# A two-layer relational graph convolution on one core: loop weights spread by DMA, both layers' edge weights from one product, one rotation of seven PSUM banks

## The chip, the cores and the metric

The kernel runs on one core of one Trainium2 chip. The core has five engines that work side by side, each through its own instructions in order: TensorE (PE; the profile lists its weight loads apart, as PEld), VectorE (DVE), ScalarE (ACT), GpSimd (POOL) and SyncE (SP), which here only issues DMAs. Engines wait for one another through semaphores. The metric is the device time of one execution in microseconds (us), lower is better.

## The reference

There are 50,000 nodes with 128 features, and 850,000 edges sorted by destination: 800,000 random ones and one self edge for each node. Every edge has one of 16 relations. Two layers follow each other, and the second has matrices of its own:

```python
W   = einsum('rb,bio->rio', w_comp, basis)         # 16 relations from 8 bases
agg = segment_sum(h[src], dst * 16 + rel, ...)     # sum of neighbours by node and relation
out = relu(einsum('nri,rio->no', agg, W) + h @ loop_w + bias)
```

The result is `layernorm(x + layer2(layer1(x)))`, all in float32. As the sums are linear, the kernel forms, for each node and each basis b, the sum over its edges of `w_comp[rel, b] * h[src]`, and multiplies that by the 8 basis matrices.

## The kernel before

**Edges.** The 800,000 real edges are cut into tiles of 128, 10 tiles to a chunk (`K`), 625 chunks in each layer. For each tile one indirect DMA on POOL (`gather`, line 247) fetches the 128 source rows into one of four row buffers of a chunk each (`GATHERS`); the gathers of chunk c+2 are issued in the code at chunk c, and a gather waits until the PE has read the tile that lay in its place, 40 tiles earlier. The PE multiplies the tile by a "hot" matrix of 128 edges x (8 bases x 12 nodes) (line 961), and DVE adds the 128 x 96 result into a ring of sums in SBUF, at an offset read from a table (`add`, line 897; the offsets come by a register load, line 891). Edge tile k is called slot k below. The adds of slot k stand in DVE's order `BEHIND` = 10 slots later. A bank of PSUM holds the products of five tiles (`PER`).

**Edge weights.** For every fourth chunk (`BATCH`) the class `Weights` loads relations and offsets (`load`, lines 632 and 636), compares them with each partition's relation on DVE (`compare`, line 648), multiplies the comparison by the layer's coefficients on the PE (`multiply`, line 655, five products of 64 columns) and copies the 320 columns to SBUF on ACT (`kept`, line 665, the single-buffered tile `pm`). `hot_of` makes the hot matrix of one chunk from `pm` (lines 870 and 877). All of this is done once in each layer.

**Groups of nodes.** Sums are taken out in groups of 512 nodes (`GN`), 98 in a layer, some 64 slots apart. The class `Group` first puts the self edge into the ring: `load` fetches the self edges' relations (line 685) and the node rows (line 694, turned on the PE, line 702, and copied by ACT, line 705) or, in layer 2, the columns stored by layer 1 (line 696); `compare` (line 713) makes a 96 x 512 comparison; then for each of the 8 bases `repeat` (line 720) multiplies it by a 96 x 128 matrix whose columns are all equal, so that every partition gets the weight of the basis for each node, and `own` (line 731) multiplies that bank of PSUM by the node's features into the ring. `planned` places the eight `repeat` steps `APART` = 5 slots apart, each `own` 10 slots behind its `repeat`. When all edges of a group are in, `copy` (line 748, ACT) takes 128 x 4096 sums out, `base` (line 754) multiplies them by the 8 basis matrices, three slots apart, `loop` (line 759) adds the self-loop matrix, `relu` (line 766) stores the columns, `back` (line 778) turns them, and `store` writes rows (layer 1, line 786) or normalizes and writes the output (layer 2).

**Order.** The order on PE, POOL, DVE and ACT is written out by hand: `later` puts a step at a slot, and the main loop runs the steps that are due. SP's order is left to a planner. Products go to two rotations of PSUM banks, `Turns`: `sums_a`, four banks, for the edge products, and `sums_o`, three banks, for everything else (`repeat`, `multiply`, `turn`, `back`). Whoever takes a bank waits until its earlier content has been read. An eighth bank holds the result of `base` and `loop`.

Of the kernel before, what the change touches and what calls it, by code (L numbers as in the profile page):

```python
# [76 lines left out]
BEHIND = 10  # L77
AFTER = 16
APART = 5
# [8 lines left out]
def tile_rgcn_resnorm(  # L88
# [43 lines left out]

    FULL = dram.tile([2 * NP, 2], F32, name="FULL")
# [17 lines left out]
    BASIS, LOOP, EACH, BIAS_OF, SPLIT = [], [], [], [], []  # L151
# [4 lines left out]
    def weighed():  # L156


        steps = consts.tile([P, AT - 1], F32, name="steps")
# [3 lines left out]
        passed = consts.tile([P, AT - 1], F32, name="passed")  # L163
        nc.vector.tensor_scalar(passed, steps, part, None, op0=OP.is_le)
        its_tile = consts.tile([P, 1], F32, name="its_tile")
# [3 lines left out]
        one_tile = consts.tile([P, AT], F32, name="one_tile")  # L169
        nc.vector.tensor_scalar(one_tile, col[:, :AT], its_tile, None, op0=OP.is_equal)  # L170
        which = consts.tile([P, PARTS], F32, name="which")
        nc.vector.tensor_scalar(which, col[:, :PARTS], its_tile, None, op0=OP.is_equal)
        again = consts.tile([P, PARTS], F32, name="again")
        nc.vector.tensor_scalar(again, col[:, PARTS : 2 * PARTS], its_tile, None, op0=OP.is_equal)
        nc.vector.tensor_add(which, which, again)
        for n, (basis, w_comp, loop_w, bias) in enumerate(GIVEN):
            bs = consts.tile([P, NB, D], F32, name=f"basis{n}")
            nc.scalar.dma_start(bs, basis.rearrange("b i o -> i b o"))
            BASIS.append(bs)
            lw = consts.tile([P, D], F32, name=f"loop{n}")  # L180
            nc.scalar.dma_start(lw, loop_w)
            LOOP.append(lw)

            ec = consts.tile([P, NB], F32, name=f"ec{n}")
# [3 lines left out]
            each = consts.tile([P, AT, NB], F32, name=f"each{n}")  # L188
            nc.vector.tensor_tensor(
                each,  # L190
# [4 lines left out]
            EACH.append(each)  # L195
# [4 lines left out]
            left, mine = ec, consts.tile([P, NB], F32, name=f"mine{n}")  # L200
            for i in range(PARTS):
                short = consts.tile([P, NB], BF16, name=f"short{n}{i}")
# [7 lines left out]
                if i + 1 < PARTS:  # L210
                    less = consts.tile([P, NB], F32, name=f"less{n}{i}")
                    nc.vector.tensor_tensor(less, left, short, op=OP.subtract)
                    left = less
            split = consts.tile([P, NB, P], BF16, name=f"split{n}")
            nc.vector.tensor_copy(split, mine[:, :, None].to_broadcast([P, NB, P]))
            SPLIT.append(split)

    ps_a = ctx.enter_context(tc.tile_pool(name="ps_a", bufs=4, space=PSUM))
    ps_o = ctx.enter_context(tc.tile_pool(name="ps_o", bufs=3, space=PSUM))
# [24 lines left out]
    sums_a, sums_o = Turns(ps_a, "pa", 4), Turns(ps_o, "po", 3)  # L244
# [6 lines left out]
    def turned(h, m, sb):  # L251

        tp = ps_o.tile([P, BANK], F32, name="po")
# [22 lines left out]
    ones = consts.tile([P, P], F32, name="ones")  # L276
# [183 lines left out]
    def rows_of(j, pool):  # L460
# [18 lines left out]
        def put(of, to):  # L479
            at = to[:, r0 * HALF : (r0 + m) * HALF].rearrange("e (r k) -> e k r", k=HALF)  # L480
            for k0 in range(0, HALF, BANK // P):
                n = min(BANK // P, HALF - k0)
                tp = sums_a.take()
# [47 lines left out]
        po = sums_o.take()  # L531
# [37 lines left out]
    def count_up(pool):  # L569
# [3 lines left out]
        total = sums_o.take()  # L573
# [26 lines left out]
    def chunked():  # L600
        with (
# [20 lines left out]
            class Weights:  # L622
# [5 lines left out]
                def load(self):  # L628
# [6 lines left out]
                    self.rel = hp.tile([P, LIVE], U8, name="rel")  # L635
# [14 lines left out]
                def multiply(self):  # L650
                    m = self.m
                    self.po = sums_o.take(self.keep)
                    of = self.po[:, :WEIGHTS].rearrange("e (t j) -> e t j", t=AT)
                    for j in range(PER):
                        nc.tensor.matmul(  # L655
                            of[:, :, j * NB : (j + 1) * NB],
                            self.is_rel[:m, j * P : (j + 1) * P],
                            EACH[self.n][:m],
                            start=True,
                            stop=True,  # L660
                        )

                def kept(self):
                    pm = hp.tile([P, WEIGHTS], F32, name="pm", bufs=1)
                    nc.scalar.copy(pm, self.po[:, :WEIGHTS])  # L665
                    self.pm = pm.rearrange("e (t b) -> e t b", b=NB)

            class Group:
                def __init__(self, g, of, n, copied):
# [3 lines left out]
                    self.each, self.made = {}, False  # L673
                    self.keep, self.kept = Once(self.turned), Once(self.store, 0)
                    self.owns = [Once(self.own, b) for b in range(NB)]

                def load(self):
                    g, n, m, cnt = self.g, self.n, self.m, self.cnt
                    if n == 0:
                        end = min(N, (g + 1) * GN)  # L680
                        while stored[0] < min(NG, -(-(end + NEAR) * E // (N * RUN * P))):
                            next(coming)
                        loaded[0] = end
# [7 lines left out]
                    self.hT = sb.tile([P, GN], F32, name="hT", bufs=4)  # L691
                    if n == 0:
                        self.h = sb.tile([P, J, D], F32, name="h_own")
                        nc.sync.dma_start(self.h[:m], of_group(self.of, g))
                    else:
                        nc.sync.dma_start(self.hT[:, :cnt], H1T[:, g * GN : g * GN + cnt])

                def turn(self):
                    m = self.m
                    self.po = sums_o.take(self.keep)  # L700
# [16 lines left out]
                def repeat(self, b):  # L717
                    cnt = self.cnt
# [465 lines left out]
```

## Time and profile before

| | |
|---|---|
| median of 3 runs (lowest to highest) | 18110.66 us (18107.38 to 18120.93) |
| profiled execution | 18092.07 us |
| its span, first to last instruction | 18090.2 us |
| mean granted TensorE clock | 0.609 |
| busy: POOL, PE, DVE, PEld, ACT | 68%, 49%, 38%, 37%, 7% |
| DMA | 1095.35 MB, mean 61 GB/s |

The profile is one execution. In its list of groups a row is: line, engine, operation, result<-operands, shape, count | busy us in all, mean ns of one | idle us of the engine just before them, and what ended most of that. "issue" is idle time in which the profile shows nothing that was waited for; "remote" is a wait whose end no recorded instruction explains. Rows of a timeline are: start in us, busy us, engine, line, operation, shapes, count, [idle before <- what ended it]. Rows of the waits are: engine and line, what it waited for, us in total, times, longest us.

### The profile page before, as it was taken

What the parts mean: (1) busy time and instruction counts of PE and PEld (TensorE: products, weight loads), DVE (VectorE), ACT (ScalarE), POOL (GpSimd) and SP (SyncE); (2) the same over time, 40 slices, a digit from 0 to 9 for tenths busy, and PEclk for the clock granted to TensorE, in tenths of its full rate; (3) what the DMA queues carried; (4) which work ended last, traced back from release to release, by engine and by line L of the source; (5) the groups of instructions that cost most, each with busy time, mean ns of one, the idle gap of its engine ahead of it and who ended that gap; (6) DMA issues with size and microseconds to landing.
All of it is one profiled execution on the core that took longest, in us unless ns stands there. A gap on an engine that the chain in (4) does not pass through costs nothing.

```text
span 18090.2 us, 137615 instructions
## 1 busy us (share of the span) xinstructions
PE 8815.7 (49%) x34524; PEld 6699.9 (37%) x34524; DVE 6821.1 (38%) x19683; ACT 1346.6 (7%) x1452; POOL 12297.6 (68%) x12540
## 2 busy tenths in 40 slices
PE   4444444544555444444444444444445444544445
PEld 3333333333333333333333333333333333333333
DVE  5444444444333333333333333333333333333333
ACT  0000000000000000000000000000000000000000
POOL 6666666666666666666666666666666666666666
PEclk6656666665665666666655666566565666666666
DMA  2222222222222222222222222222222222222222
GB/s 78 68 69 64 68 69 68 68 63 62 59 59 58 59 59 59 59 58 59 57 55 58 58 59 58 58 58 59 58 58 58 59 58 59 59 59 59 58 58 54
DMA packets 568561, 1095.35 MB, mean 61 GB/s; under 512 B 218506, under 2 KB 262764, under 8 KB 567756
## 3 DMA queue, kind: packets, MB, share of 16 engines
q0 software_dynamic: 403552, 826.82, 18.9%
q1 hardware_dynamic: 161276, 258.45, 4.4%
q8 instruction: 282, 4.62, 0.1%
q14 instruction: 523, 4.28, 0.1%
q10 hardware_dynamic: 2928, 1.19, 0.0%
HBM read 987.64 MB, written 97.93 MB: 60 GB/s over the span
## 4 chain that ended last, share of the span: by engine, by line
issue 39%; PE 28%; another core or an unknown queue 15%; DVE 8%; POOL 6%; DMA 2%; ACT 1%; DVEq 1%; POOLq 0%; ACTq 0%; SPq 0%
PE pa L961 16%; PE pn L754 7%; POOL g L247 6%; DVE ring L897 4%; PE po L655 2%; DVE ring L731 2%; PE po L720 1%; DMA g<-in_x_dram,src 1%; DVEq L891 1%; DMA g<-H,src 1%; ACT own L748 1%; PE po L778 1%; PE pn L759 1%; DVE own L870 0%
## 5 line engine op out<-in xcount | busy, mean ns | idle before, releaser
L961 PEld LDWEIGHTS pa<-hot,g 128*128 128x128 f32 x25000 | 5222.6, 274 | 8042.2 <-issue 7000.4
L247 POOL DMA_INDIRECT g<-in_x_dram,src x6250 | 6140.9, 983 | 2844.0 <-issue 1397.4
L247 POOL DMA_INDIRECT g<-H,src x6250 | 6120.1, 979 | 2864.0 <-issue 1410.5
L961 PE MATMUL pa<-hot,g 128*128 128x96 f32 x25000 | 5476.4, 355 | 4369.5 <-issue 3768.7
L897 DVE TENSOR_TENSOR ring<-pa,ring 128x96 f32 x12500 | 3205.9, 256 | 10795.4 <-remote 5049.8
L754 PE MATMUL pn<-own,basis 128*128 128x512 f32 x3104 | 2296.2, 818 | 529.6 <-issue 515.5
L720 PE MATMUL po<-is_lrel,split 96*128 96x512 bf16 x1568 | 797.8, 510 | 2312.8 <-issue 903.2
L877 DVE TENSOR_TENSOR hot<-pm,own 128x960 f32<-128x960 f32 x1250 | 1451.4, 1161 | 81.1 <-ACT pm L665 13.8
L655 PE MATMUL po<-each,is_rel 128*128 128x64 f32 x3140 | 671.9, 375 | 1159.1 <-issue 727.1
L731 DVE TENSOR_TENSOR ring<-po,hT 128x512 f32<-128x512 f32 x1568 | 1078.8, 689 | 110.8 <-remote 29.5
L655 PEld LDWEIGHTS po<-each,is_rel 128*128 128x128 f32 x3140 | 625.5, 289 | 1209.5 <-issue 747.3
L748 ACT COPY own<-ring 128x4096 f32<-128x4096 f32 x194 | 699.5, 3606 | 3877.3 <-DVE ring L897 2158.7
L754 PEld LDWEIGHTS pn<-own,basis 128*128 128x128 f32 x3104 | 668.4, 253 | 768.6 <-issue 766.5
L665 ACT COPY pm<-po 128x320 f32<-128x320 f32 x314 | 133.5, 425 | 6635.0 <-DVE hot L877 2743.9
L778 PE MATMUL po<-ident,oT 128*128 128x128 f32 (+1 forms) x784 | 205.6, 397 | 650.2 <-DVE ring L731 388.9
L778 PEld LDWEIGHTS po<-ident,oT 128*128 128x128 f32 (+1 forms) x784 | 143.8, 220 | 684.2 <-issue 537.3
L720 PEld LDWEIGHTS <-split 96*128 96x128 bf16 x1568 | 236.0, 151 | 388.0 <-issue 387.5
L766 ACT ACTIVATE oT<-pn,bias_of 128x512 f32<-128x512 f32 x196 | 134.7, 687 | 3019.6 <-PE pa L961 1597.5
L870 DVE TENSOR_TENSOR own<-col,key 128x120 bf16<-128x120 f32 x1250 | 346.4, 277 | 0.5
L759 PE MATMUL pn<-hT,loop 128*128 128x512 f32 x392 | 265.6, 759 | 32.5 <-issue 32.2
L326 DVE COPY_PREDICATED word<-bit,word 128x224 int32<-128x224 int32 (+9 forms) x450 | 181.2, 403 | 16.1 <-DVE bit L323 0.8
L648 DVE TENSOR_SCALAR is_rel<-rel,its_rel 128x640 f32<-128x640 uint8 x314 | 181.3, 578 | 0.1
(126 smaller groups left out, 1497.1 us busy)
## 6 DMA issues: line engine op xcount, KB each, us to landing
g<-in_x_dram,src POOLq DMA_INDIRECT x6250
g<-H,src POOLq DMA_INDIRECT x6250
lrel<-LREL SPq DMA_DIRECT2D x194, 192.0 KB
rel<-REL SPq DMA_DIRECT2D x312, 80.0 KB
h_own<-in_x_dram SPq DMA_DIRECT2D x97, 256.0 KB
xw<-in_x_dram SPq DMA_DIRECT2D x97, 256.0 KB
H1T<-oT SPq DMA_DIRECT2D x97, 256.0 KB
H<-t SPq DMA_DIRECT2D x97, 256.0 KB
```

Source lines behind the costliest of these rows:

```text
L247: return nc.gpsimd.indirect_dma_start(out=to, out_offset=None, in_=of, in_offset=bass.IndirectOffsetOnAxis(ap=idx, axis=0))
L655: nc.tensor.matmul(of[:, :, j * NB : (j + 1) * NB], self.is_rel[:m, j * P : (j + 1) * P], EACH[self.n][:m], start=True, stop=True,)
L720: nc.tensor.matmul(self.each[b][:, :cnt], SPLIT[self.n][:LOOPS, b, :], self.is_rel[:LOOPS, :cnt], start=True, stop=True,)
L731: nc.vector.tensor_tensor(ring[:, b, self.at : self.at + cnt], self.each.pop(b)[:, :cnt], self.hT[:, :cnt], op=OP.mult,)
L748: nc.scalar.copy(self.sums, ring[:, :, at : at + cnt])
L754: nc.tensor.matmul(self.pn[:, : self.cnt], BASIS[self.n][:, b, :], self.sums[:, b, :], start=b == 0, stop=False)
L759: nc.tensor.matmul(self.pn[:, : self.cnt], LOOP[self.n], self.hT[:, : self.cnt], start=False, stop=True)
L778: nc.tensor.transpose(self.po[:m, j * D : (j + 1) * D], by_place[:, j, :], ident)
L870: nc.vector.tensor_tensor(own[:, : ks(c)], grid[:, None, :].to_broadcast([P, ks(c), WN]), key[:, c * K : c * K + ks(c), None].to_broadcast ...
L877: nc.vector.tensor_tensor(hot[:, : ks(c)], pm[:, c % BATCH * K : c % BATCH * K + ks(c), :, None].to_broadcast([P, ks(c), NB, WN]), own[:, ...
L897: nc.vector.tensor_tensor(into, pa[:, k % PER * NB * WN : (k % PER + 1) * NB * WN].rearrange("d (b w) -> d b w", w=WN), into, op=OP.add,)
L961: nc.tensor.matmul(pa[:, k % PER * NB * WN : (k % PER + 1) * NB * WN], g[:, k, :], hot[:, k].rearrange("e b w -> e (b w)"), start=True, st ...
```

## The change

Self-edge weights: one product for each group, made in layer 1 alone, gives 16 rows (8 bases of both layers) x 512 nodes (`combine`). ACT copies them, SP stores them to DRAM (`CW`), and in both layers SP loads four bases at a time back, each row repeated over 128 partitions (`widen`, into a tile with a single buffer, `WIDE` = 1). `own` then multiplies four bases at once, from SBUF. Edge weights: in layer 1 each product has the columns of both layers (128 in place of 64) and fills two banks, ACT makes four copies, and the part of layer 2 goes to DRAM (`PM2`), from where layer 2 loads it; layer 2 makes no comparison and no product of its own. PSUM: one rotation of seven banks for all. `BASIS` and `LOOP` have one buffer and are loaded again for layer 2. `BEHIND` is 12 and `AFTER` is 18 (16 before); `base` steps are two slots apart. Core of the diff:

```diff
-BEHIND = 10
-AFTER = 16
-APART = 5
+BEHIND = 12
+AFTER = 18
+AT_ONCE = 4
+WIDE = 1
+PARTS_OF = ((0, 3), (3, 5))
...
-    sums_a, sums_o = Turns(ps_a, "pa", 4), Turns(ps_o, "po", 3)
+    banks = Turns(ps_a, "pa", 7)
...
 class Weights: def load
+    if self.n:
+        pm = hp.tile([P, WEIGHTS], F32, name="pm")
+        nc.sync.dma_start(pm, PM2[c // BATCH * P : (c // BATCH + 1) * P, :])
+        return
...
 def multiply
-    self.po = sums_o.take(self.keep)
+    self.po = [banks.take(self.keep) for _ in PARTS_OF]
...
 def kept
+    for n in range(2):
+        for po, (j0, j1) in zip(self.po, PARTS_OF):
+            nc.scalar.copy(...)
+        if n:
+            nc.sync.dma_start(PM2[c * P : (c + 1) * P, :], pm)
...
 class Group:
-    def repeat(self, b):
+    def combine(self):
+        nc.tensor.matmul(self.comb[: 2 * NB, : self.cnt],
+            split[:LOOPS].rearrange("r n b -> r (n b)"), self.is_rel[:LOOPS, : self.cnt], ...)
+    def stored_comb(self):
+        nc.scalar.copy(comb[:, :cnt], self.comb[: 2 * NB, :cnt])
+        nc.sync.dma_start(CW[:, at : at + cnt], comb[:, :cnt])
+    def widen(self, b):
+        self.wide[b] = sb.tile([P, AT_ONCE, GN], F32, name="wide", bufs=WIDE)
+        nc.sync.dma_start(self.wide[b][:, :, : self.cnt], bass.AP(tensor=CW.tensor, ...,
+            ap=[[0, P], [NGR * GN, AT_ONCE], [1, self.cnt]]))
     def own(self, b):
-        nc.vector.tensor_tensor(ring[:, b, ...], self.each.pop(b)[:, :cnt], self.hT[:, :cnt], op=OP.mult)
+        nc.vector.tensor_tensor(ring[:, b : b + AT_ONCE, ...], self.wide.pop(b)[:, :, :cnt],
+            self.hT[:, None, :cnt].to_broadcast([P, AT_ONCE, cnt]), op=OP.mult)
...
 def planned
-    went = start - APART * NB - BEHIND
-    later(went - 28, self.load)
-    for b in range(NB):
-        later(went + APART * b, self.repeat, b)
-        later(went + APART * b + BEHIND, self.owns[b])
+    went = start - 2
+    if self.n == 0:
+        later(went - 78, self.load)
+        later(went - 66, self.turn)
+        later(went - 62, self.compare)
+        later(went - 48, self.combine)
+        later(went - 48 + BEHIND, self.combined)
+    else:
+        later(went - 40, self.load)
+    for i, b in enumerate(range(0, NB, AT_ONCE)):
+        later(went - 30 + 14 * i, self.widen, b)
+        later(went - 16 + 14 * i, self.own, b)
-        later(end + AFTER + 3 * b, self.base, b)
+        later(end + AFTER + 2 * b, self.base, b)
...
+    if n:
+        later(30, matrices, 1, nc.sync)
```

More of the change, by code (lines that the diff above doesn't have):

```diff
@@ L690, in load @@
                     )
[L691 to L696, printed above, removed]
+                    self.h = sb.tile([P, J, D], F32, name="rows")
+                    nc.sync.dma_start(self.h[:m], of_group(self.of, g))
                 def turn(self):
                     m = self.m
-                    self.po = sums_o.take(self.keep)
+                    self.po = banks.take(self.keep)
                     for j in range(J):
```

183 lines of the change are left out of this document (103 added, 80 removed).

## The prediction

> **What bounds the kernel now.** I read the groups by cost first.
>
> ```profile
> span 18090.2 us, 137615 instructions
> L247 POOL DMA_INDIRECT g<-in_x_dram,src x6250 | 6140.9, 983 | 2844.0 <-issue 1397.4
> L247 POOL DMA_INDIRECT g<-H,src x6250 | 6120.1, 979 | 2864.0 <-issue 1410.5
> L877 DVE TENSOR_TENSOR hot<-pm,own 128x960 f32<-128x960 f32 x1250 | 1451.4, 1161 | 81.1 <-ACT pm L665 13.8
> L655 PE MATMUL po<-each,is_rel 128*128 128x64 f32 x3140 | 671.9, 375 | 1159.1 <-issue 727.1
> L731 DVE TENSOR_TENSOR ring<-po,hT 128x512 f32<-128x512 f32 x1568 | 1078.8, 689 | 110.8 <-remote 29.5
> L720 PE MATMUL po<-is_lrel,split 96*128 96x512 bf16 x1568 | 797.8, 510 | 2312.8 <-issue 903.2
> L778 PE MATMUL po<-ident,oT 128*128 128x128 f32 (+1 forms) x784 | 205.6, 397 | 650.2 <-DVE ring L731 388.9
> ```
>
> POOL's 12,500 gathers are the longest row. Next I read one gather by itself, from its source line, and its pace in a timeline.
>
> ```profile
> L247 POOL DMA_INDIRECT g<-in_x_dram,src x6250: 938/945/1929, 45.8 to 9064.3; - x196
> L247 POOL DMA_INDIRECT g<-H,src x6250: 938/945/1932, 9099.2 to 18049.3; - x196
> ```
> ```profile
> 12006.27 1.16 DVE L877 TENSOR_TENSOR hot<-pm,own 128x960 f32<-128x960 f32 x1
> 12006.54 1.71 POOL L247 DMA_INDIRECT g<-H,src  x1 [0.30 <-issue]
> ...
> 12017.29 0.95 POOL L247 DMA_INDIRECT g<-H,src  x1 [0.30 <-issue]
> 12018.54 0.94 POOL L247 DMA_INDIRECT g<-H,src  x1 [0.30 <-issue]
> ```
>
> Undisturbed, a gather starts every 1.25 us (0.95 and 0.30). POOL's floor is then 12,500 x 1.25 = 15,625; plus gathers stretched beyond their median, (983 - 945) x 6250 + (979 - 945) x 6250 ns = 450; plus 46 before the first, 35 between the layers (9064.3 to 9099.2) and 41 after the last: 16,197 us. The span is 18,090. So POOL spends about 1,890 us waiting, and that is all that any change which leaves the gathers alone can win. For whom does it wait?
>
> ```profile
> PEld pa L961 <- issue: 7000.4, 6266, 37.7
> POOL g L247 <- remote: 1229.4, 1060, 5.4
> POOL g L247 <- PE pa L961: 1204.3, 1538, 6.8
> PEld pa L961 <- DMA g<-in_x_dram,src: 221.3, 127, 17.4
> PEld pa L961 <- DMA g<-H,src: 201.4, 120, 17.9
> ```
>
> POOL waits for the PE to free row buffers, while the PE hardly waits for gathered rows (221 + 201). So the PE runs behind, with the 40 row tiles nearly full, and it sets the pace. It is not the PE's work: it idles 2312.8 + 1159.1 + 650.2 = 4,122 us before the three operations that take a bank of the three-bank rotation (L720, L655, L778 above). There is a second loss, which no wait explains. Timeline, start of layer 2:
>
> ```profile
> 9150.77 0.32 PE L961 MATMUL pa<-hot,g 128*128 128x96 f32 x1 [2.48 <-issue]
> ...
> 9152.18 0.29 PEld L961 LDWEIGHTS pa<-hot,g 128*128 128x128 f32 x1 [2.52 <-issue]
> ...
> 9153.57 0.32 PE L961 MATMUL pa<-hot,g 128*128 128x96 f32 x1 [2.48 <-issue]
> ```
>
> For tens of us the PE takes one instruction every 1.4 us, with nothing it waits for. Most of the 7,000 us "issue" above is of this kind; its cause I can't see.
>
> **The change part by part.** Sums are against the profiled span; the profiled execution (18,092.07) lies 2 above the span and 18.6 below the median.
>
> *`repeat` goes.* Off the PE: 1,568 products, 798 us, and the 2,313 idle before them; 98 `combine` products at some 0.5 us come in, 50.
>
> *Edge weights of layer 2 go.* Half of L655: (672 + 1,159) / 2 = 915 us of PE. Layer 1's products get 128 columns for 64. No row has that width in float32; the bounds are no change (375 ns) and L754's 128x512 float32 product at 818 ns, so 0 to (818 - 375) x 1,570 = 700 us; I take 100, near the lower end, because L961's 96 columns already cost no more (355 ns) than L655's 64:
>
> ```profile
> L754 PE MATMUL pn<-own,basis 128*128 128x512 f32 x3104 | 2296.2, 818 | 529.6 <-issue 515.5
> L961 PE MATMUL pa<-hot,g 128*128 128x96 f32 x25000 | 5476.4, 355 | 4369.5 <-issue 3768.7
> ```
>
> *Seven banks.* An edge bank is held 5 + 12 = 17 slots and was 5 + 10 = 15 of the four banks' 20. Layer 1 now takes, in 64 slots, 12.8 edge banks, 3.2 for weights and 3 for turn, combine and back: 7 of 19 is 23.6 slots. Layer 2 takes 13.8: 32.5 slots. DVE's slack rises from 5 slots to 6.6 and 15.5. Of what idles before L655 and L778 and is not yet counted, 580 + 650, I take half: 615. In all the PE is spared 3,111 - 50 + 915 - 100 + 615 = 4,490 us: its own path falls to some 13,600, below POOL's floor.
>
> *`own` on DVE.* 1,568 x 689 ns go (1,079). 392 operations of 128x2048, all operands in SBUF, come.
>
> ```profile
> L742 DVE TENSOR_TENSOR ring<-ring 128x96 f32<-128x96 f32 x64 | 16.5, 258 | 2.2
> ```
>
> From 96 to 960 columns (L742, L877) a column costs (1161 - 258) / 864 = 1.045 ns, so 2048 cost 2.30 us: 902 in all. DVE, busy for 6.8 ms, gains little; the cost is POOL's. L877 reads two SBUF operands, and the gather that starts under it above took 1.71 instead of 0.95. Charging all 450 us of stretch to L877's 1,451 busy us gives 0.31 us of POOL per us; for 902 that is 280. The ends are 0 and 902; I take 280, measured on the same kind of operation.
>
> The Trainium skill ("SBUF — State Buffer", section "Who interferes with whom") says that a DVE instruction with two SBUF inputs shares a read interface with GpSimd, and that the later of the two blocks fully until the other ends; one with a single SBUF input does not contend. The trace agrees in kind (1.71 us); a full block would charge 902, which is a rival below.
>
> *Other work moved.* ACT makes four copies for one in layer 1, none in layer 2:
>
> ```profile
> L665 ACT COPY pm<-po 128x320 f32<-128x320 f32 x314 | 133.5, 425 | 6635.0 <-DVE hot L877 2743.9 <-issue 2269.0 <-PE pa L961 1048.8
> L786 ACT COPY t<-po 128x512 f32<-128x512 f32 x98 | 57.3, 585 | 725.8 <-remote 414.2 <-PE pa L961 287.3 <-PE po L778 14.6
> ```
>
> At (585 - 425) / 192 = 0.83 ns a column, 192 and 128 columns cost 319 and 266 ns: 157 x 1,170 ns = 184 us for 134. The 98 copies of `comb` add 57. ACT idles far more (6,635 before L665 alone): nothing. `pm` now has two buffers, so the copy no longer waits for L877 (2,744). The denser `base` steps move PE work, and remove none: 0.
>
> *The new chain.* `widen` is issued 14 slots, 17.5 us, before `own`; the single buffer lets the second start only after the first `own`, again 14 slots before its own. SP gets 392 loads of 1.05 MB.
>
> ```profile
> q0 software_dynamic: 403552, 826.82, 18.9%
> q1 hardware_dynamic: 161276, 258.45, 4.4%
> ```
>
> SP's queue moves 258 MB in 4.4% of 16 x 18,090 us, 20.3 KB per us and engine. So 1.05 MB takes 65.5 / 20.3 = 3.2 us, some 4 beside gathers that hold 18.9%. Issue and landing are bounded by layer 2's first gather, whose product starts 2.9 us after its issue:
>
> ```profile
> 9099.22 1.23 POOL L247 DMA_INDIRECT g<-H,src  x1 [33.09 <-DMA H<-t]
> ...
> 9102.15 0.71 PE L961 MATMUL pa<-hot,g 128*128 128x96 f32 x2 [5.56 <-DMA g<-H,src]
> ```
>
> About 7 us of 17.5, then: 10.5 us of cover, and `widen` costs nothing while SP is on time. At a layer's start nothing covers it: two loads in series and a store, some 15 us for each layer, 30. If the cover is gone, rival 3 prices it. SP's other edits: layer 2's loads of relations (98 L685, 157 L636) go, 157 loads of `pm` and 157 + 98 stores come; all move a tenth of what `widen` does, on an SP that mostly waits: 0.
>
> The Trainium skill ("DMA: Bandwidth & Descriptors", section "Measured") has 6.15 us for a load of 1 MB, which would leave some 11 us of cover; no run here has shown a load of that size.
>
> *What POOL still waits.* With the PE's path at 13,600 of 16,500 instead of all of it, stretches of 1.4 us steps longer than the 40 row tiles still stop POOL. Ends are 0 and today's 1,890; I take a quarter, 475, since PE and POOL would no longer be equal.
>
> Sum: 16,197 + 280 + 30 + 475 = 16,982 of span; with 2 and 18.6 about 17,000 us, 6% less.
>
> **The rivals.**
>
> 1. *The PE's 1.4 us steps take back what is freed.* For: most of the 7,000 us "issue" has no visible cause, and steps packed closer may bring more. Against: they come after waits, too. If two thirds of POOL's 1,890 stay: 16,197 + 280 + 30 + 1,260 + 21, about 17,790.
>
> 2. *POOL shut out for the whole of each `own`:* 902 instead of 280, 17,620. Against: L877's 1,451 us stretch gathers by 450 at most. (This is the skill's rule above, taken to its full.)
>
> 3. *Slower: `widen` is late because SP is.* SP issues in order and stands in long waits:
>
> ```profile
> SPq L768 <- ACT oT L766: 1916.2, 61, 52.6
> SPq L696 <- PE pa L961: 1793.1, 57, 59.8
> SPq L632 <- DVEq L891: 1743.9, 97, 63.5
> ```
>
> These are 31, 31 and 18 us each, more than the 10.5 of cover. DVE then stands at `own`, with every add and hot matrix queued behind it; the adds free the banks, so the PE stops, then POOL. A group has 92 us today (18,090 / 196) and 87 in my forecast, of which the PE could use 18%, 16 us, to catch up. Break-even is two lost stretches of (5 + 16) / 2 = 10.5 us a group, past bank slack of 6.6 and 15.5 slots (8 and 19 us): loads 10.5 + 8 + 10.5 = 29 us late in layer 1, 40 in layer 2. Each us more costs 2 x 196 = 392 us; 2 us past that point give 18,900. For: the waits above. Against: they are mostly SP arriving early, and the planner orders SP by when each DMA can go.
>
> 4. *No change:* POOL's "remote" waits are something else than the PE's. Then 18,090.
>
> **How the numbers follow.** Chances: forecast 0.54 (16,390 to 17,450), rival 1 0.18, rival 2 0.08, rival 3 0.17, rival 4 0.03. A measurement here can tell 0.2% from no change. Faster takes the forecast and rivals 1 and 2: 0.80; same 0.03; slower 0.17. The low end is the floor with nothing for `own` and a tenth of the waits, 16,197 + 189, about 16,390; 0.05 may lie below it. The high end reaches past rivals 1, 2 and 4 into the first of rival 3, 18,250, and leaves some 0.15 above.
>
> **What would show it.** No L720; POOL's idle before L247 near 2,150 a layer instead of 2,850, with "PE pa L961" and "remote" much smaller; PE waiting for gathered rows (DMA g) more than 420 us; `own` about 2.3 us x392 with little wait for the wide tile; layer 2 shorter than layer 1. Wrong if DVE's rows at `own` wait hundreds of us for the load (rival 3), if L247's mean passes 1,040 ns (rival 2), or if PEld's "issue" grows beyond 7,000 us (rival 1).

## The result: 0.2% slower, and the profile after

The kernel after took 18147.89 us (median of 20 runs, 18121.82 to 18180.86), the kernel before 18106.9 (20 runs beside them, 18090.17 to 18120.93). The ratio is 1.0023, with a 95% interval of 1.0016 to 1.003. The forecast was 17,000 us, 6% less. The whole range, 16,390 to 18,250 us, holds the measured time only because its upper end had been set past the rivals.

From the page of the kernel after: the span, then the groups that answer to those shown of before.

```profile
span 18141.6 us, 132343 instructions
L1004 PE MATMUL pa<-hot,g 128*128 128x96 f32 x25000 | 5869.2, 361 | 8329.8 <-issue 5856.8
L250 POOL DMA_INDIRECT g<-in_x_dram,src x6250 | 6497.8, 1040 | 2549.3 <-issue 1150.2
L250 POOL DMA_INDIRECT g<-H,src x6250 | 6426.4, 1028 | 2549.6 <-issue 1167.7
L789 PE MATMUL pn<-own,basis 128*128 128x512 f32 x3104 | 2062.1, 749 | 242.5 <-issue 193.9
L916 DVE TENSOR_TENSOR hot<-pm,own 128x960 f32<-128x960 f32 x1250 | 1457.5, 1166 | 90.8 <-remote 17.5
L766 DVE TENSOR_TENSOR ring<-wide,hT 128x2048 f32<-128x2048 f32 x392 | 896.1, 2286 | 232.3 <-DMA wide<-CW 111.9
L664 PE MATMUL pa<-each,is_rel 128*128 128x128 f32 x1570 | 375.3, 376 | 579.6 <-issue 380.6
L813 PE MATMUL pa<-ident,oT 128*128 128x128 f32 (+1 forms) x784 | 215.5, 378 | 236.2 <-issue 190.1
```

The gathers by themselves in the kernel after (min/median/max ns, first and last start), and its waits:

```profile
L250 POOL DMA_INDIRECT g<-in_x_dram,src x6250: 939/947/3060, 46.0 to 9117.1; - x196
L250 POOL DMA_INDIRECT g<-H,src x6250: 939/947/3058, 9152.5 to 18093.2; - x196
```
```profile
PEld pa L1004 <- issue: 7601.0, 7243, 47.2
PEld pa L1004 <- DMA g<-H,src: 870.5, 858, 6.1
PEld pa L1004 <- DMA g<-in_x_dram,src: 576.4, 598, 6.5
POOL g L250 <- remote: 1076.3, 727, 7.9
POOL g L250 <- PE pa L1004: 717.3, 1335, 7.4
```

The change did on the PE what it says. L720 is gone, and the idle before weights and `back` fell from 1,159 and 650 us to 580 and 236. But the PE's idle before the edge products grew from 4,370 to 8,330 us: what was freed came back there, about half of it as "issue" (3,769 to 5,857).

POOL's account, built as in the prediction: 12,500 x 1.25 = 15,625; stretch (1040 - 947) x 6250 + (1028 - 947) x 6250 ns = 1,087.5; 46.0 + 35.4 + 48.4 at the ends. That is 16,842.3, so 1,299 of the span of 18,141.6 are waits. Against before (18,090 - 16,197 = 1,893), the waits fell by 594 us and the stretch rose by 638. The pace, 1.45 us a gather, is what it was.

Two things were to be explained: why POOL got only a third of its waits back, and why the gathers were stretched by 638 us more, where 280 were forecast.

### The profile page after: what moved, and what is told of

Same layout as the page of the kernel before. It is cut to its first block, busy times and chain, and to the rows that moved or that the text cites. A ratio compares the mean times of both kernels' runs of the same rounds, so it can differ in the third digit from the quotient of the medians.

```text
span 18141.6 us, 132343 instructions
## 1 busy us (share of the span) xinstructions
PE 8301.5 (46%) x31484; PEld 6157.8 (34%) x31484; DVE 6520.1 (36%) x18252; ACT 1406.4 (8%) x1864; POOL 12963.3 (71%) x12540
## 4 chain that ended last, share of the span: by engine, by line
issue 37%; PE 22%; another core or an unknown queue 15%; POOL 14%; DMA 7%; DVE 3%; ACT 1%; DVEq 0%; POOLq 0%; ACTq 0%; SPq 0%
PE pa L1004 14%; POOL g L250 14%; PE pn L789 5%; DMA g<-H,src 4%; DMA g<-in_x_dram,src 3%; DVE ring L936 1%; PE pa L664 1%; ACT own L783 1%; PE pa L813 1%; PE pn L794 1%; DVE ring L766 1%; DVE word L329 0%; DVE bit L326 0%; DVEq L930 0%
## 5 line engine op out<-in xcount | busy, mean ns | idle before, releaser
L1004 PE MATMUL pa<-hot,g 128*128 128x96 f32 x25000 | 5869.2, 361 | 8329.8 <-issue 5856.8
L250 POOL DMA_INDIRECT g<-in_x_dram,src x6250 | 6497.8, 1040 | 2549.3 <-issue 1150.2
L250 POOL DMA_INDIRECT g<-H,src x6250 | 6426.4, 1028 | 2549.6 <-issue 1167.7
L789 PE MATMUL pn<-own,basis 128*128 128x512 f32 x3104 | 2062.1, 749 | 242.5 <-issue 193.9
L766 DVE TENSOR_TENSOR ring<-wide,hT 128x2048 f32<-128x2048 f32 x392 | 896.1, 2286 | 232.3 <-DMA wide<-CW 111.9
L664 PE MATMUL pa<-each,is_rel 128*128 128x128 f32 x1570 | 375.3, 376 | 579.6 <-issue 380.6
L664 PEld LDWEIGHTS pa<-each,is_rel 128*128 128x128 f32 x1570 | 312.7, 273 | 631.9 <-issue 467.7
L813 PE MATMUL pa<-ident,oT 128*128 128x128 f32 (+1 forms) x784 | 215.5, 378 | 236.2 <-issue 190.1
L813 PEld LDWEIGHTS pa<-ident,oT 128*128 128x128 f32 (+1 forms) x784 | 147.8, 221 | 279.2 <-issue 271.5
L601 ACT ACTIVATE t<-t,nm,rs 128x128 f32<-128x128 f32 x392 | 161.3, 482 | 78.3 <-issue 36.1
```

The costliest lines, as they stand in the source:

```text
L250: return nc.gpsimd.indirect_dma_start(out=to, out_offset=None, in_=of, in_offset=bass.IndirectOffsetOnAxis(ap=idx, axis=0))
L664: nc.tensor.matmul(of[:, :, :, (j - j0) * NB : (j - j0 + 1) * NB], self.is_rel[:m, j * P : (j + 1) * P], each[:m], start=True, stop=True,)
L766: nc.vector.tensor_tensor(ring[:, b : b + AT_ONCE, self.at : self.at + cnt], self.wide.pop(b)[:, :, :cnt], self.hT[:, None, :cnt].to_broad ...
L789: nc.tensor.matmul(self.pn[:, : self.cnt], BASIS[:, b, :], self.sums[:, b, :], start=b == 0, stop=False)
L813: nc.tensor.transpose(self.po[:m, j * D : (j + 1) * D], by_place[:, j, :], ident)
L1004: nc.tensor.matmul(pa[:, k % PER * NB * WN : (k % PER + 1) * NB * WN], g[:, k, :], hot[:, k].rearrange("e b w -> e (b w)"), start=True, st ...
```

## The experiments

The runs fell on several chips, and that turned out to matter. They are named here by letters, with the time of the kernel before on each. Which chip A is was not noted; it need not be a chip of its own. The diffs show the main lines; `...` stands for others. no_gathers, fixed_rows, sp_loads, pool_fill and narrow were run once on each chip named, so they have no interval.

| chip | A (the result) | B | C | D | E | F |
|---|---|---|---|---|---|---|
| before, us | 18,107 | 18,273 | 16,171 | 16,171 | 18,271 | 16,186 |

A "step" below is a pair of successive starts on the PE (weight load or product) that lie a multiple of 0.70 us (up to 2.8) apart, within 0.035 us; their sum is given per run. A kernel that is free of long rows of steps shows 0.2 to 1.0 ms of such pairs. The kernel before on A has 5.8 ms, after 7.3.

### Are the bank waits the lever? (chip B)

**b_banks7**, on the kernel before:

```diff
-    ps_a = ctx.enter_context(tc.tile_pool(name="ps_a", bufs=4, space=PSUM))
-    ps_o = ctx.enter_context(tc.tile_pool(name="ps_o", bufs=3, space=PSUM))
+    ps_a = ctx.enter_context(tc.tile_pool(name="ps_a", bufs=7, space=PSUM))
...
-    sums_a, sums_o = Turns(ps_a, "pa", 4), Turns(ps_o, "po", 3)
+    sums_a = sums_o = Turns(ps_a, "pa", 7)
...
-went = start - APART * NB - BEHIND
+went = start - APART * NB - BEHIND - 6
...
+if c == 0:
+    go_on(-1)
```

> The kernel before with one part of the change alone: the four banks of pa and the three of po become one rotation of seven, and the loop weights' products are put 6 steps earlier so that the order still holds; the 776 repeats and the second layer's weights stay. The result is the same. If PE's waits for a bank (4,122 us before L720, L655 and L778) set the pace, as the prediction had it, half of them go and the whole falls by 400 us or more, below 17,700 us. If PE's slow steps take back whatever is freed (rival 1), the pace stays: 17,950 to 18,250 us.

18,266 us; ratio to before 0.9998 (0.9989 to 1.0008). That is 16 us over its range, which was set by the times on A. Groups of b_banks7:

```profile
L962 PE MATMUL pa<-hot,g 128*128 128x96 f32 x25000 | 5706.2, 355 | 5761.8 <-issue 4768.0
L719 PE MATMUL pa<-is_lrel,split 96*128 96x512 bf16 x1568 | 791.4, 507 | 1168.4 <-issue 496.8
L654 PE MATMUL pa<-each,is_rel 128*128 128x64 f32 x3140 | 687.3, 358 | 905.8 <-issue 720.6
L777 PE MATMUL pa<-ident,oT 128*128 128x128 f32 (+1 forms) x784 | 222.1, 391 | 386.6 <-issue 279.4
```

Beside before on chip A, the idle before the three operations that take a bank of `sums_o` fell from 4,122 to 2,461 us, the idle before the edge products rose by 1,392, and the time stayed; its trace has 7.8 ms of steps. (The kernel before has no trace from B.) Bank waits are not what sets the pace.

### What does the PE need alone, and beside gathers? (chip B, then F)

**no_gathers** and **fixed_rows**, on the kernel after:

```diff
-for k in range(ks(to)):
+for k in range(ks(to) if n * C + to < GATHERS else 0):
```
```diff
-buffer = (n * C + to) % GATHERS
+buffer = 1 + (n * C + to) % (GATHERS - 1) if n or to else 0
...
-g = rows[(n * C + c) % GATHERS]
+g = rows[0]
```

> The kernel after, but only the first 40 of the 12,500 gathers are issued; the products read those rows again and again, so the sums are of the wrong rows. All work of PE, DVE, ACT and SP stays. If PE's slow steps come from its own work (its rate of instructions, its clock), they stay, several ms of them, and the whole takes over 15,000 us. If they need the gathers beside them (their writes to SBUF, their descriptors), they are gone and the whole falls to 9,500 to 12,500 us: PE's busy 8,300 us, its weight loads partly beside them, and DVE's 6,500 us busy with the waits between.

> The kernel after, but the products of the edges (L1004) all read one row tile that is filled once, while all 12,500 gathers still run, into the other three row tiles, which nobody reads: the sums are of the wrong rows. POOL no longer waits for PE, and PE no longer for gathers; work and traffic stay. Theory A, the gather path itself makes the pace of 1.447 us a gather: POOL's gathers still end at about 9,100 us in layer 1, and the whole takes 18,000 to 18,200 us. Theory B, PE's slow steps make the pace (1.4 us an instruction with no wait recorded, 7.3 ms of the 18.1 in the kernel after): POOL runs ahead, its layer takes 6,250 x 1.25 us + about 560 us of stretched gathers = 8,400 us or less, and the whole still takes 17,600 to 18,200 us, since PE's slow steps stay. Theory C, neither, only the coupling over 40 row slots costs (a slow stretch of PE stops POOL, and PE then waits for POOL): the whole falls to 16,800 to 17,300 us.

no_gathers took 8,642 us, 858 under its range, with 0.2 ms of steps: all of the other engines' work fits in less than half of the time. fixed_rows took 23,312 us, more than any theory had, with 13.6 ms of steps. Where POOL runs free, the PE falls back until the gathers have ended. Windows of fixed_rows, of 1 ms each (PE, PEld, DVE, ACT, POOL busy us and instructions, clock, DMA share, GB/s): in the first two POOL gathers, in the third it has finished.

```profile
12000.00:13000.00 1000.00, 144.56 (x357) 101.81 (x357) 79.17 (x227) 14.41 (x19) 759.65 (x714) 0.50 0.19 55
15000.00:16000.00 1000.00, 148.64 (x357) 102.20 (x358) 73.88 (x217) 14.42 (x19) 759.68 (x715) 0.50 0.18 54
20600.00:21600.00 1000.00, 756.73 (x3564) 592.91 (x3562) 750.37 (x2142) 147.71 (x163) 0.00 (x0) 0.73 0.22 75
```

Timeline of fixed_rows inside such a stretch:

```profile
14990.85 0.29 PEld L1004 LDWEIGHTS pa<-hot,g 128*128 128x128 f32 x1 [2.51 <-issue]
14991.85 1.09 POOL L250 DMA_INDIRECT g<-H,src  x1 [0.30 <-issue]
14992.25 0.32 PE L1004 MATMUL pa<-hot,g 128*128 128x96 f32 x1 [2.48 <-issue]
14993.25 1.09 POOL L250 DMA_INDIRECT g<-H,src  x1 [0.30 <-issue]
14993.65 0.29 PEld L1004 LDWEIGHTS pa<-hot,g 128*128 128x128 f32 x1 [2.51 <-issue]
14993.67 1.43 DVE L936 TENSOR_TENSOR ring<-pa,ring 128x96 f32 x5 [22.89 <-remote]
```

In this kernel the PE waits for no gather after the first chunk, and still it does 357 weight loads and 357 products of all kinds in 1 ms while gathers run, and 3,564 products when they have ended. The steps are those of the prediction's 1.4 us: a weight load, a product, a weight load. DVE runs its adds at full speed once it has something to add. The half clock (0.50) stands beside a PE that is busy for 145 us of 1,000, and this run can't tell which follows from which.

The first window shows more: 357 + 357 PE instructions, and 714 gathers. From 12 to 20 ms it is 5,713 PE instructions and 5,713 gathers, one for one, one of each in 1.40 us. So POOL is slowed as well. It waits for nothing there, and a gather takes 1.07 us in the mean (6,084 us in 5,713) and not 0.945, with DVE busy for 8% of the time. That is why layer 2's gathers took 8,728 us where 8,400 or less were expected of a POOL that runs free.

**fixed_rows_2** is the same kernel on chip F:

> The kernel of fixed_rows once more (the gathers run, nobody waits for them or reads them; the sums are of the wrong rows). Where before takes over 18,000 us: 23,000 to 23,600 us again, PE at one instruction in 1.4 us for as long as POOL runs free. Where before takes about 16,200 us, on a chip without such steps: PE and DVE are done long before POOL, and the whole takes POOL's floor, 15,900 to 16,900 us.

17,006 us there, 100 over the expected range, and 0.3 ms of steps. One window of it:

```profile
5000.00:6000.00 1000.00, 789.15 (x4242) 636.00 (x4241) 746.67 (x2034) 187.52 (x282) 797.63 (x665) 0.79 0.43 130
```

4,242 products beside 665 gathers in 1 ms: on this chip the PE isn't held up.

### Transfers, or POOL's work? (chips C and E)

**sp_loads** and **pool_fill**, on fixed_rows, for all gathers from the second chunk on:

```diff
-gather(rows[buffer][:, k, :], of, src[:, to * K + k : to * K + k + 1])
...
+nc.sync.dma_start(rows[buffer][:, k, :], x[at : at + P, :])
```
```diff
-gather(rows[buffer][:, k, :], of, src[:, to * K + k : to * K + k + 1])
...
+nc.gpsimd.memset(rows[buffer][:, : K - 1, :], 0.0)
```

> The kernel after, but from the second chunk on each gather is replaced by a plain load of 128 rows (the same 64 KB in 128 rows of 512 B) on SP's queue, into row tiles that nobody reads; the products read one row tile filled once, so the sums are of the wrong rows. The bytes that land in SBUF stay (819 MB), POOL issues nothing. If the transfers slow PE, PE's 1.4 us steps are there and the whole takes well over 12,000 us. If it is what POOL does for a gather (writing the descriptors), they are gone and it takes 8,700 to 11,000 us, a little more than the 8,642 us without any.

> The kernel after, but from the second chunk on each gather is replaced by a fill of 1,152 elements a partition on POOL, back to back, into row tiles that nobody reads; the products read one row tile filled once, so the sums are of the wrong rows. POOL is about as busy and issues no gathers. With free gathers instead of the fills the same kernel took 23,312 us, with neither 8,642 us. If it is POOL's being busy that slows PE to one instruction in 1.4 us, this takes over 15,000 us, with several ms of such steps. If it is the gathers' descriptors or transfers, the steps are gone and it takes 8,600 to 9,500 us (or as long as POOL's fills).

They took 10,180 and 13,956 us, without steps, but on C, where the kernel before has none to speak of, so this told nothing of the cause. They were run again on E, where before takes 18,271.

> The kernel of sp_loads once more: from the second chunk on each gather is replaced by a plain load of 64 KB on SP's queue, the products read one row tile filled once, the sums are of the wrong rows. Where before takes about 16,200 us this can tell nothing of PE's steps, and it takes 10,180 us again. Where before takes over 18,000 us: if the transfers cause PE's steps, there are over 1 ms of them in the trace and it takes over 11,500 us; if the gathers' descriptors or POOL do, there are none in runs and it takes 10,000 to 10,500 us.

> The kernel of pool_fill once more: from the second chunk on each gather is replaced by a fill on POOL, back to back, no transfer; the products read one row tile filled once, the sums are of the wrong rows. Where before takes about 16,200 us it takes 13,950 us again (POOL's fills set the end, PE is done at about 9,800). Where before takes over 18,000 us: if POOL's being busy is enough for PE's steps, PE is done only after 13,000 us and has several ms of them; if not, PE is done at 9,500 to 10,500 us with steps of under 0.5 ms in all.

10,162 and 13,957 us, each with 0.3 ms of steps. One window of sp_loads_2, then one of pool_fill_2:

```profile
5000.00:6000.00 1000.00, 647.71 (x3161) 511.56 (x3161) 591.92 (x1635) 127.16 (x171) 0.00 (x0) 0.71 0.59 169
```
```profile
7000.00:8000.00 1000.00, 766.34 (x3564) 597.15 (x3565) 750.60 (x2153) 149.68 (x168) 952.76 (x907) 0.72 0.23 76
```

With three times the DMA traffic of fixed_rows the PE does 3,161 products in 1 ms, and beside a POOL that is busy for 953 of 1,000 us it does 3,564. So on such a chip neither plain transfers by themselves nor POOL's being busy brings the steps; it takes a gather. Which part of one does it isn't shown. (The plain loads read rows that follow each other, the gathers read scattered ones; no run kept the scatter and left POOL out.)

The traces of the kernels in which the PE does wait for gathers tell when the slow stretches begin and end. A slow stretch is counted here as an unbroken row of steps of 6 us and longer.

```
starts of stretches per ms outside of them, by gathers started in the last 10 us
                        5      6      7      8
before (A)            0.7    0.0   10.3   34.8
after (A)             0.0    1.1    7.1   40.8
own_psum (B)          0.0    0.3   16.3   55.1
gathers begun in a stretch: share with which it ended before the next gather,
by the time to that next gather
                   under 1.3 us    4 to 6 us
before (A)              3%             90%
after (A)               1%             61%
own_psum (B)            4%             76%
```

Slow stretches begin after an unbroken run of gathers, and they tend to end in a pause of some us, which POOL makes when the 40 row tiles are full. If this is cause and effect, the pace holds itself: whatever lets POOL run longer without a break brings the next stretch sooner. The runs fit this reading, but it is not shown, as no run paced the gathers on purpose.

### What stretches the gathers (chips B, D and E)

Timeline of POOL, then of DVE, in the kernel after:

```profile
9315.51 0.95 POOL L250 DMA_INDIRECT g<-H,src  x1 [1.93 <-remote]
9316.77 2.34 POOL L250 DMA_INDIRECT g<-H,src  x1 [0.31 <-issue]
9319.41 0.94 POOL L250 DMA_INDIRECT g<-H,src  x1 [0.30 <-PE pa L1004]
```
```profile
9315.99 2.29 DVE L766 TENSOR_TENSOR ring<-wide,hT 128x2048 f32<-128x2048 f32 x1
9324.19 1.16 DVE L916 TENSOR_TENSOR hot<-pm,own 128x960 f32<-128x960 f32 x1
```

The gather that runs when `own` starts isn't touched; the next one, begun at 9316.77, ends 0.83 us after `own` has (9319.11 against 9318.28). So it is in the whole trace: the gather that runs when `own` starts has a median of 0.95 us, the one begun under it 2.51, and that one ends 0.81 to 0.82 us after `own` in nine of ten cases. Giving each stretched gather of the trace to the DVE operation that overlaps it most, `own` costs 576 us in 378 gathers, 1.5 us each, and `hot` 470 (336 in before).

The Trainium skill ("SBUF — State Buffer", section "Who interferes with whom") says that a DVE instruction with two SBUF inputs contends with a GpSimd instruction that reads SBUF, and that one with at most one SBUF input, outside of DVE's two-port modes, doesn't. The gathers read their row numbers from SBUF. The next two kernels agree with it.

**own_psum** (on the kernel after) and **all_psum** (on own_psum):

```diff
...
+def lift(self):
+    self.up = banks.take(self.both)
+    nc.scalar.copy(self.up[:, : self.cnt], self.hT[:, : self.cnt])
...
-self.hT[:, None, :cnt].to_broadcast([P, AT_ONCE, cnt])
+self.up[:, None, :cnt].to_broadcast([P, AT_ONCE, cnt])
...
+later(went - 24, self.lift)
```
```diff
-banks = Turns(ps_a, "pa", 7)
+banks = Turns(ps_a, "pa", 6)
...
+owns = ps_w.tile([P, BANK], F32, name="owns")
...
-own = hp.tile([P, K, WN], BF16, name="own")
+own = owns[:, c % 2 * K * WN : (c % 2 + 1) * K * WN].rearrange("p (k w) -> p k w", k=K)
...
+if c == 0:
+    go_on(-1)
```

> The kernel after, but ACT first copies hT to a PSUM bank of the rotation (97 copies a layer) and own (L766) reads it there, so that it has one SBUF operand and one in PSUM. The result is the same. If own's two SBUF operands are what stretches the gathers (their mean 1,040 and 1,028 ns now, about 0.945 us unstretched, 1,113 us in all, 450 us before the change), the mean falls to about 980 ns, 660 us less busy time. Rival 2 of the prediction: the whole falls by 300 to 660 us, to 17,500 to 17,850 us. Rival 1: POOL waits for PE instead and the whole stays within 100 us of 18,150 us. If the two operands don't matter, the means stay over 1,020 ns.

On B: 18,193 us, ratio to before 0.9964 (0.995 to 0.9978); 8.2 ms of steps. Its gathers:

```profile
L250 POOL DMA_INDIRECT g<-in_x_dram,src x6250 | 6162.4, 986 | 2877.4 <-issue 1309.3
L250 POOL DMA_INDIRECT g<-H,src x6250 | 6140.1, 982 | 2878.9 <-issue 1248.1
```

Beside the kernel after on A (it did not run on B), `own`'s stretch is gone (the means fell by 54 and 46 ns, 622 us less busy time) and all of it came back as idle (328 + 329 us). Where the steps are, stretch and waits trade against each other.

The next four ran on D, where the kernel before takes 16,171 us.

> The kernel before, unchanged, once more on another chip, for its trace. On the chips of the first runs it took 18,107 and 18,273 us, on the chip of the last ones 16,171 us, which is POOL's floor as the prediction worked it out (16,197 us). Theory A, PE's slow steps belong to the chip and not to the kernel: where the time is about 16,200 us, the trace has hardly any steps of 1.4 us, PE's busy time is much the same and POOL's waits are under 100 us; where the time is over 18,000 us, the trace has over 4 ms of them. Theory B, the times differ for another reason (shorter gathers, faster loads): the gathers' mean or gap differs from 0.985 and 0.30 us.

> The kernel after, unchanged, on the same chip. Theory A: on a chip where before takes about 16,200 us, POOL is at its floor and the change shows its own price there, the gathers stretched by own (576 us by the trace of the kernel after: 378 gathers that meet L766 by 1.5 us each) and by hot (470 against 336 us): 16,800 to 17,000 us, 4 to 5% slower. On a chip where before takes over 18,000 us, the two are within 0.5% of each other again. Theory B, the change is neutral wherever it runs: within 1% of before on either.

> The kernel after with own reading hT from PSUM, on the same chip. Theory A: where before takes about 16,200 us, this takes 16,150 to 16,350 us, since the 576 us of stretched gathers are gone (its gathers' mean was 984 ns, before's 985 ns); so it is within 1% of before and 3.5% or more faster than after. Where before takes over 18,000 us, within 1% of both.

> As own_psum, and the second operand of hot (L916 of the kernel after) is put in a PSUM bank too, so that neither of DVE's long products has two operands in SBUF; the rotation has six banks instead of seven, and the first group's events run ahead of the first product. The result is the same. The stretched gathers that meet hot (463 us in own_psum) go as well: the gathers' mean is below 960 ns. Theory A: where before takes about 16,200 us, the whole takes 15,700 to 15,900 us, 2 to 3% faster than before; where before takes over 18,000 us, the pace stays and it is within 1% of before. If PSUM operands don't matter for hot, the mean stays at about 984 ns and the time that of own_psum.

| on chip D | us | ratio to before (95%) | steps, ms |
|---|---|---|---|
| before_again | 16,164 | | 0.5 |
| after_again | 16,913 | 1.0456 (1.0438 to 1.0473) | 0.4 |
| own_psum_again | 16,442 | 1.017 (1.0153 to 1.0187) | 0.4 |
| all_psum | 15,827 | 0.9787 (0.9771 to 0.9804) | 0.4 |

Gathers of before_again, after_again, own_psum_again and all_psum, layer 1 each:

```profile
L247 POOL DMA_INDIRECT g<-in_x_dram,src x6250 | 6116.5, 979 | 1934.7 <-issue 1085.9
```
```profile
L250 POOL DMA_INDIRECT g<-in_x_dram,src x6250 | 6503.3, 1041 | 1941.2 <-issue 1169.7
```
```profile
L250 POOL DMA_INDIRECT g<-in_x_dram,src x6250 | 6209.6, 994 | 1943.3 <-issue 1143.4
```
```profile
L252 POOL DMA_INDIRECT g<-in_x_dram,src x6250 | 5944.3, 951 | 1952.6 <-issue 1142.6
```

The idle is 0.31 us a gather in all four: POOL hardly waits, and the time is its busy time. In before_again it is the PE that waits, for rows:

```profile
PEld pa L961 <- DMA g<-H,src: 3365.4, 3914, 4.4
PEld pa L961 <- DMA g<-in_x_dram,src: 3044.0, 3555, 4.9
PEld pa L961 <- issue: 902.6, 1391, 25.6
```

"issue" is 903 us against 7,000 on A. So theory A holds in what matters: gathers are as long as on A (median 944 ns), the steps are missing, POOL's waits are 25 us by the account above, and the change costs 4.6%. It missed that the PE's products are longer here (415 ns a product of edges, 355 on A), which costs nothing, as the PE waits for rows. The mean granted clock of the kernel before is 0.625 here and 0.609 on A, a difference of 2.6% beside 12% in time, so the clock alone does not make it. own_psum_again missed its range by 92 us, and it is 2.8% faster than after where 3.5% were expected: without `own`'s stretch, `hot` meets more gathers (612 us, 552 in after_again). all_psum came out as theory A had it and beats both kernels: with one operand in PSUM in both products the stretch is down to 54 us.

> The kernel of all_psum once more (own and hot each with one operand in PSUM), in the hope of a chip on which before takes over 18,000 us. If the 1.4 us steps of PE come whenever gathers follow each other without a break (their start was 10 times likelier after 8 gathers in 10 us than after 5 or 6), quicker gathers only bring more of them: the pace stays at 1.44 to 1.46 us a gather and the whole within 1% of before. If they come at a rate of their own, the 450 us of stretches saved stay saved: 17,600 to 17,800 us. Where before takes about 16,200 us: 15,830 us again.

On E, with steps, all_psum_2 took 18,216 us, ratio to before 0.9968 (0.9955 to 0.998), with 7.2 ms of steps and gathers of 950 and 944 ns. The pace is 1.46 us a gather, as was expected if the steps come with unbroken gathers. It beats before on both kinds of chip, by 2.1% and by 0.3%.

### Bytes and passes (chips C and F)

**narrow** (from the fifth chunk on) and **half_pe**, both on the kernel after, and **half_all** (all_psum with half_pe's edit):

```diff
-gather(rows[buffer][:, k, :], of, src[:, to * K + k : to * K + k + 1])
...
+gather(rows[buffer][:, k, :32], of.rearrange("n (q d) -> (n q) d", d=32), src[:, to * K + k : to * K + k + 1])
```
```diff
-hot = hp.tile([P, K, NB, WN], F32, name="hot", bufs=4)
+hot = hp.tile([P, K, NB, WN], BF16, name="hot", bufs=4)
...
-g[:, k, :],
+g[:, k, :].bitcast(BF16)[:, 1::2],
```

> The kernel after, with every gather at its place, waited for and read, but each brings 128 rows of 32 numbers instead of 128 (16 KB instead of 64 KB, 128 descriptors as before): the rest of each row tile is old, so the sums are wrong. If the bytes moved cause PE's steps or hold the pace of 1.447 us, the whole falls to 16,500 to 17,300 us (12,500 x 1.25 us and the stretched gathers). If the number of gathers and descriptors does, it stays at 17,900 to 18,300 us.

> The kernel after, but hot is made in bf16 and the products of the edges read the upper halves of the gathered numbers, so each takes one pass instead of two: 12,500 weight loads and products instead of 25,000; the sums are rounded to about 8 bits of mantissa. Gathers, DVE and ACT stay. If PE advances by one instruction in 1.4 us beside the gathers, it now needs 2.8 us instead of 5.6 for a gather's rows in such a stretch, falls behind less and POOL waits less: POOL's waits (1,290 us) go for the most part and the whole falls to 16,800 to 17,500 us. If the pace of 1.447 us a gather is POOL's or the transfers' own, it stays within 100 us of 18,150 us.

> The kernel of all_psum, and as in half_pe hot is made in bf16 and the products of the edges read the upper halves of the gathered numbers: 12,500 weight loads and products instead of 25,000, the sums rounded to about 8 bits of mantissa. Where before takes over 18,000 us: if PE advances by one instruction in 1.4 us in its slow stretches, it needs 2.8 us for a gather's rows there instead of 5.6, falls behind half as fast, and POOL waits much less: 16,300 to 17,300 us (all_psum took 18,216 there). If the pace of 1.45 us a gather is not PE's, 18,100 to 18,300 us. Where before takes about 16,200 us: POOL's floor, 15,800 to 15,850 us, as all_psum.

> The kernel of narrow once more (each gather brings 16 KB instead of 64 KB in as many descriptors; the sums are wrong). Where before takes about 16,200 us it takes 16,910 us again, as after does there. Where before takes over 18,000 us: if the bytes of the gathers bring PE's steps, it is at 16,900 to 17,300 us with steps of under 2 ms in all; if the descriptors do, it stays at 17,900 to 18,300 us.

All four ran on chips without steps. A quarter of the bytes: 16,909 and 16,880 us, against 16,913 of the kernel after on D. Half of the PE's passes: half_pe 16,940 us, ratio to before 1.0474 (1.0456 to 1.0491). half_all 15,863, 13 over its range, ratio 0.9799 (0.9782 to 0.9815). So at POOL's floor neither the bytes of a gather nor the PE's work counts, and half_pe's 16,940 us, inside the range that was to speak for the steps, speaks for nothing but the floor. What halved passes or fewer bytes do on a chip with the steps was not measured.

## Why the prediction was wrong, step by step

**POOL's floor, 16,197 us: right.** On D and C the kernel before runs at it (16,164 and 16,171).

**"It sets the pace", of the PE: right on A; the 4,122 us of idle before the three operations that take a bank as the cause: wrong.** The profile had put 1,746 of these us (903, 727 and 115) down to "issue", and so to no bank. b_banks7 took away 1,661 us of that idle and nothing of the time. The idle stood in a PE that was late anyway, because of the 1.4 us steps.

**The PE spared 4,490 us, "its own path falls to some 13,600": this step failed.** A path summed from idle and busy rows assumed that the rest, the steps, would stay as long as they were. They did not: they went from 5.8 to 7.3 ms, PEld's "issue" from 7,000 to 7,601 us (the mark set for rival 1), and the idle before the edge products by 3,960. Without gathers the whole kernel takes 8,642 us, far less than 13,600; beside free ones it takes 23,312. So what the PE needs on such a chip is set by the gathers beside it, and no sum of its own rows gives it.

**"I take a quarter, 475", POOL's remaining waits: 1,299.** That is close to the 1,260 of rival 1. PE waits for rows rose from 423 to 1,447 us as foreseen, so it did catch up at times, and then fell back.

**`own`: its length was right, its price not.** 2,286 ns against 2.30 us forecast; 576 us of stretch against 280, and `hot` 134 us more. The price was taken as a share of `hot`'s busy time. But the gather begun under such an operation waits for its whole rest; of a short one most falls on the gather already running and the 0.30 us gap, of a 2.29 us one 1.5 us are left. The last is argued from these lengths. Rival 2 named the full block, with 902 us as its end; its mark, a mean of over 1,040 ns, was met in layer 1 (1,040) and not passed.

**Widen, the copies, SP: right.** DVE waited 112 us in all for the wide tile; rival 3 didn't come. But layer 2 gained little: 8,941 us from its first gather to its last (8,950 before), and layer 1 lost, 9,071 (9,018 before).

So what happened on A is rival 1 and part of rival 2 together: 594 us less waiting and 638 more stretch. The forecast left out that the two are not independent there (own_psum), and, on chips without the steps, that there were no waits to win at all. That they nearly cancel fits own_psum, where the stretch that was removed came back as waits. What in a gather holds the PE stays open.

## What to carry to other kernels

Before an engine's idle time is counted as gain, find out what that engine needs with the suspected neighbour taken away: here 8,642 us without gathers and 23,312 with free ones said more than any sum of rows. If POOL's indirect DMAs are the bound, give DVE's long two-operand products one operand in PSUM. On D that took the kernel after from 16,913 to 16,442 us, 1.2 us for each of the 392 products of 2.29 us; on the chips with the steps it was worth next to nothing. Measure on more than one chip: the same change cost 0.2% on one and 4.6% on another.

## What the runs showed of the hardware

- The kernel before takes 16,171 to 16,186 us on C, D and F and 18,107 to 18,273 on A, B and E, with gathers of the same length (medians 944 ns on D and 945 on A). Each was used on one occasion, so that it is the chip and not the moment isn't shown.
- On chips of the second kind gathers slow a PE that waits for nothing: 357 products in 1 ms instead of 3,564, one PE instruction for each gather, with a gather every 1.40 us instead of 1.25. The Trainium skill ("SBUF — State Buffer", section "Who interferes with whom") says that PE and ACT never wait on anyone. fixed_rows differs; whether it is over SBUF that the PE is held up, no run shows.
- Plain loads from SP, at three times the traffic, and fills on POOL don't do that on a chip of this kind (3,161 and 3,564 products in 1 ms on E; fixed_rows ran on B).
- A gather begun under a 2.29 us product of two SBUF operands ends 0.82 us after it; with one operand of `own` and of `hot` in PSUM the stretch of all gathers is 54 us (all_psum) and not 1,148 (after_again). A gather of a quarter of the bytes takes as long (median 944 ns in narrow).
